# The high and low parts of two FFN weights, made and stored in earlier stages of a two-layer FFN kernel

## The chip, the cores and the metric

The kernel runs on one core of one Trainium2 chip. The metric is the device time of one execution in microseconds (us). The engines of the core are named as in the profile: PE is TensorE (matmuls and transposes), PEld its weight loads, DVE is VectorE, ACT is ScalarE, POOL is GpSimd, and SP is SyncE, which here issues nearly all DMAs, in the order of its own instruction list. Every engine takes its instructions in order: an instruction that waits holds all that stand behind it on its engine.

## The reference

The input is 2 x 1024 rows of 1024 numbers in float32. There are two layers, each followed by a residual addition and a layer norm. The first is a gated FFN in which, of each row's 2752 gate values, the 1376 of least magnitude are set to zero. The second is a gated FFN with weights that are repeated four times and have a small correction of rank 2.

```python
s = silu(x @ w_gate.T)                      # 2048 x 2752
s = s with the I/2 smallest |s| of each row set to 0
x = layernorm(x + (s * (x @ w_up.T)) @ w_down.T)

def lin(x, wq, A, B):                       # w = tile(wq, (1, 4))
    return x @ w.T + (x @ A.T @ B.T) * 0.5
h = silu(lin(x, w1q, a1, b1)) * lin(x, w3q, a3, b3)
x = layernorm(x + lin(h, w2q, a2, b2))
```

## The kernel before

**Tiles and precision.** The 2048 rows are 16 tiles of 128 rows, in four groups of four. A float32 operand is split into a high part (a cast to the rounded type fp32r, on ACT, line 172) and a low part (operand minus high part, on POOL or DVE, line 173), and a product is made of three matmuls: high by high, high by low, low by high. A weight that several groups use is split once; its parts are stored to device memory, and later groups load the two parts instead of the raw weight.

**Stages, in order of time.** `gate_up` makes the gate and up products of all groups. `topk` finds each row's threshold by a search that counts on ACT and DVE; the counting of a group runs beside the matmuls of later work, and that of the last group runs during `down`. `down(g)`, for g from 0 to 3, makes the down product of one group, the residual and the layer norm. It is a loop over six stretches of the 2752 columns (512, 512, 512, 384, 384, 448) and the four tiles of the group, 24 items in all. `ffn(g)` then makes the second layer of one group: f1, eight blocks of 344 hidden columns by four tiles (the four repeated quarters of the weight allow it to work on the rows folded to 256 columns), and f2, the product with w2.

**An item of down.** `item` (the call in `down`) issues the loads of an item, does its preparation two items later and its matmuls three items after that. The loads are m (the gate times up values, line 699), u (the mask of the topk, line 700) and, at the first item of a stretch, the stretch's weight rows (`down_w`): either stored parts (line 673) or a raw row (line 600) that is split. ACT turns u to bf16 (701), POOL multiplies m by it (702), PE transposes m (723), ACT and DVE make the high and low parts mh and ml of the transposed tile (727, 728), and the matmuls run at line 743. DVE adds their sum to acc (746), which frees the PSUM buffer. After a tile's last stretch the layer norm runs on DVE with one instruction on POOL (y, line 577), and the tile goes to device memory (765).

**The critical section.** At the end of a topk DVE reads a flag and may branch to an exact search. Around that branch all engines have a branch of their own, DVE waits there for the work that was issued earlier, DMAs too, and no DMA is issued by SP in the meantime. The last of these sections falls into down(2).

**f1 and its weights.** `f1_prep` gets for each block the parts wh and wl of w1 and w3, 344 KB each, from four buffers of each kind. In group 0, `cached` loads the raw weight to a ring of three buffers (`wr`, which the rows of w_down and w2 use also), splits it, with the low part of w3 on DVE and that of w1 on POOL, and `cache_put` stores both parts; groups 1 to 3 load the parts. The five rows of w2 go the same way in f2. A block's matmuls are lines 959 to 962, its epilogue is silu on ACT (965), the product on DVE (966), the products with a2 (pa, DVE 968) and their sums (ACT 970), and on POOL the sum of the folded quarters (hf, 972). Before a tile's f1 its rows are folded on POOL (905 to 907), and fold and the small tile tl are transposed on PE (927, 929). `ffn_consts` and `f1_first` prepare the first FFN group's constants and tiles during down(3).

**Order.** The Python code gives the order in which instructions are recorded; a scheduler then orders each engine's list by a timeline of its own and the pools' free buffers. `load_behind()` keeps a load behind the last load of down on SP, and `behind()` keeps an instruction behind the last mh and ml on ACT and DVE. Generators such as `topk`, `dots_down` and `ffn_consts` are advanced a step at a time by the items of `down`.

Of the kernel before, what the change touches and what calls it, by code (L numbers as in the profile page):

```python
# [7 lines left out]
F = mybir.dt.float32  # L8
R = mybir.dt.float32r
# [4 lines left out]
ALU = mybir.AluOpType  # L14
# [4 lines left out]
P = 128  # L19
# [5 lines left out]
BW = 344  # L25
NB = NI // BW
# [6 lines left out]
GT = 4  # L33
# [32 lines left out]
class Kern:  # L66
# [7 lines left out]
    def run(self):  # L74
        tc, nc = self.tc, self.nc
        nt = self.nt
        ng = nt // GT
        with ExitStack() as es:
# [51 lines left out]
            self.acc = Ring("acc", [(self.dp2, f"acc{i}", H) for i in range(5)] + [(dp3, f"acc{i}", H) for i in range(5, 8)], F)  # L130
            for r, n in ((self.wh, "wh"), (self.wl, "wl")):
                r.slots += [(self.wp2, n + "x", H), (self.dp2, n + "y", H), (dp3, n + "z", H)]
            list(self.d0)
            for g in range(1, ng - 1):
                list(self.down(g))
            list(self.dg)
            for r in (self.acc, self.wh, self.wl):
                r.drop(dp3)
# [275 lines left out]
    def topk(self, g, nact=3):  # L414
        nc, tk, sm = self.nc, self.tk, self.sm
        V = nc.vector
        tiles = range(g * GT, (g + 1) * GT)
        row = lambda n, dt=F, bufs=2: sm.tile([P, GT], dt, tag="k" + n, bufs=bufs, name=n)
# [4 lines left out]
        b = ku.rearrange("p a n -> p (a n)").bitcast(F)  # L423
        jk = tk.tile([P, NI], U8, tag="jk", name="jk")
        asum, d = row("asum"), row("d")
        lo, hi, cur = pair("lo"), pair("hi"), pair("cur")
# [23 lines left out]
        for p in range(NPASS):  # L450
            for j in range(nact):
# [3 lines left out]
                with self.behind():  # L455
                    t, s = cur[:, 0, j : j + 1], cur[:, 1, j : j + 1]
                    nc.scalar.activation(jk.bitcast(I8), av[j], AF.Sign, bias=t, scale=-1.0, accum_out=s)  # L457
                    if m < GT:
                        t, s = cur[:, 0, m : m + 1], cur[:, 1, m : m + 1]
# [14 lines left out]
            t = nxt[:, 0]  # L474
# [36 lines left out]
                    kv[j], av[j], thr[:, j : j + 1], None, ALU.is_ge, ALU.add, accum_out=cnt[:, j : j + 1]  # L511
                )
        yield
        bad, fl, ft = row("bad"), sm.tile([P, 32], F, tag="kfl", bufs=1, name="fl"), sm.tile([P, 32], F, tag="kft", bufs=1, name="ft")
        V.tensor_scalar(bad, cnt, float(NI - KZ), None, ALU.not_equal)
        V.memset(fl, 0.0)
        V.tensor_reduce(fl[:, 0:1], bad, mybir.AxisListType.X, ALU.max)
# [1 line left out]
        fr, f4 = sm.tile([P, 1], F, tag="kfr", bufs=1, name="fr"), sm.tile([1, 4], F, tag="kf4", bufs=1, name="f4")  # L519
# [85 lines left out]
    def down(self, g, f1=None, early=0):  # L605
        n = 0
        for ib in range(len(DB)):
            if f1 is not None:
                if ib == f1:
                    self.fg = self.f1_first()  # L610
            ws = []
            for t in range(g * GT, (g + 1) * GT):
                st = {"e": n} if n < early else {}
                load = lambda: self.down_load(st, ib, t, n)
                prep = lambda st=st, ib=ib: self.down_prep(st, ib)
                mm = lambda st=st, ib=ib, t=t, ws=ws: self.down_mm(st, ib, t, ws)
                if n < early:
                    load()
                    prep()
                    self.q2.append(mm)  # L620
                    if n == early - 1:
                        yield
                else:
                    self.item(lambda: (load(), self.down_w(g, ib, ws)), prep, mm, 2, 3)
                n += 1
                if g == 0 and n == 12:
                    self.tkg = self.topk(self.nt // GT - 1, 2)
                if (n > 11 or g) and self.tkg and next(self.tkg, 1):
                    self.tkg, self.dg = None, self.dots_down()
                if f1 is not None and n > 4:  # L630
                    next(self.fcg, None)
                    if ib >= f1:
                        next(self.fg, None)
                for _ in range(2 if n % 2 else 1):
                    next(self.dg, None)
        if f1 is not None:
            list(self.fg)
        yield
# [180 lines left out]
    def ffn_consts2(self):  # L819
        nc, fp2, A = self.nc, self.fp2, self.A  # L820
        self.c2 = True
        self.c2h = fp2.tile([P, H], R, name="c2h")
        self.c2l = fp2.tile([P, H], R, name="c2l")
        raw = self.wr.get()
        nc.gpsimd.memset(raw[96:P, :H], 0.0)
        nc.sync.dma_start(raw[0:48, :H], A["w2t"][640:688, :])
        nc.sync.dma_start(raw[48:96, :H], A["w2t"][640:688, :])
        for i in range(2):
            nc.sync.dma_start(raw[96 + 2 * i : 98 + 2 * i, :H], A["b2t"])
        self.split(self.c2h, self.c2l, raw[:, :H])  # L830

    def ffn(self, g):
        tiles = [t for t in range(g * GT, (g + 1) * GT) if t < self.nt]
        for b in range(NB):
            ws = []
            if tiles[-1] + 1 < self.nt:
                if b % 2 == 0:
                    if b:
                        self.f1_tile2(tiles[-1] + b // 2)
                    self.f1_tile(tiles[-1] + 1 + b // 2)  # L840
            for t in tiles:
                self.item(
                    lambda: self.f1_prep(b, ws),
                    lambda: None,
                    lambda st=self.fst[t], b=b, ws=ws: self.f1_mm(st, b, ws),
                    2, 2,
                )
        if tiles[-1] + 1 < self.nt:
            self.f1_tile2(tiles[-1] + GT)
        ws = []  # L850
        for t in tiles:
            self.item(
                lambda: self.f2_w(ws),
                lambda t=t: self.f2_prep(self.fst[t], t),
                lambda st=self.fst[t], t=t, ws=ws: self.f2_mm(st, t, ws),
                2, 1,
            )
# [212 lines left out]
```

## Time and profile before

| what | us |
|---|---|
| three runs | 1931.73, 1930.43, 1925.01 |
| their median | 1930.43 |
| the profiled execution | 1929.24 |
| its span in the trace | 1927.4 |
| TensorE busy in the span | 1885.9 |
| DMA engines, share of the span | 71.9% |

The page cuts the span into 40 equal slices of 48.2 us. Each digit is a share in tenths (9 is 90% or more); the row PEclk is the clock that TensorE was granted.

```profile
PE   9999999999999999999999999999999999998998
DVE  4633555767358474691237996778558757779565
PEclk9999999999999999999999999999999999999999
DMA  7667697676967868667797756877776878485661
GB/s 270 236 248 262 231 328 259 214 274 253 331 227 244 313 243 297 233 221 255 277 345 271 281 188 233 308 254 261 280 240 248 269 285 322 157 317 177 226 199 66
```

By the first and last matmuls of each kind in the trace, gate_up ends at 933 us, down(0) to down(3) run from there to 1471, and the four FFN groups from 1467 to 1919: f1 of group 0 until 1553, its f2 until 1594, f1 of group 1 until 1665, and so on. So a stage is several slices long, and its numbers are read from windows of its own.

### The profile page before, as it was taken

The page shows a single profiled execution, that of the slowest core. Times are in us where ns is not written, and L with a number is a line of the kernel's source. Part 1 is how long each engine was busy: PE and PEld are TensorE (multiplying, and loading weights), DVE is VectorE, ACT ScalarE, POOL GpSimd, SP SyncE. Part 2 cuts the span into 40 slices and gives each one's busy share as a digit, 9 for nine tenths or more (in the row PEclk, how much of TensorE's full clock was granted, in tenths as well). Part 3 has the DMA queues.
Part 4 walks back from the last instruction along what each step waited for, and adds up shares of the span by engine and source line. Part 5 has one row for each costly group of instructions (what it writes and reads, how often), then busy time and mean ns, then how long its engine had stood idle before and what let it go on. Part 6 is the DMA issues. An engine that isn't in the chain of part 4 may idle for free. (4 is left out here: it accounts for less than half of the span.)

```text
span 1927.4 us, 29369 instructions
## 1 busy us (share of the span) xinstructions
PE 1885.9 (98%) x10825; PEld 1755.3 (91%) x10825; DVE 1229.5 (64%) x1831; ACT 905.5 (47%) x1448; POOL 974.0 (51%) x606
## 2 busy tenths in 40 slices
PE   9999999999999999999999999999999999998998
PEld 9999999999999999999887887788877979898896
DVE  4633555767358474691237996778558757779565
ACT  4333478414882258612246532323333746567362
POOL 5665664435445354355555543545655746436062
PEclk9999999999999999999999999999999999999999
DMA  7667697676967868667797756877776878485661
GB/s 270 236 248 262 231 328 259 214 274 253 331 227 244 313 243 297 233 221 255 277 345 271 281 188 233 308 254 261 280 240 248 269 285 322 157 317 177 226 199 66
DMA packets 166205, 488.66 MB, mean 254 GB/s; under 512 B 24772, under 2 KB 45380, under 8 KB 166056
## 3 DMA queue, kind: packets, MB, share of 16 engines
q1 hardware_dynamic: 165848, 486.43, 71.9%
q8 instruction: 85, 1.39, 0.3%
q14 instruction: 64, 0.52, 0.1%
q10 hardware_dynamic: 208, 0.31, 0.0%
HBM read 370.30 MB, written 116.33 MB: 252 GB/s over the span
## 5 line engine op out<-in xcount | busy, mean ns | idle before, releaser
L173 POOL TENSOR_TENSOR wl<-wr,wh 128x1376 fp32r<-128x1376 f32 (+2 forms) x187 | 566.7, 3038 | 430.1 <-ACT wh L172 411.7
L350 PE MATMUL mm<-wh,xh 128*128 128x344 f32 x1928 | 611.1, 322 | 3.5 <-DMA wh<-tw3T1h 3.5
L350 PE MATMUL mm<-wh,xl 128*128 128x344 f32 x1928 | 610.4, 320 | 0.0
L172 ACT CAST wh<-wr 128x1376 fp32r<-128x1376 f32 (+2 forms) x192 | 232.1, 1215 | 300.7 <-PE mm L350 181.7
L350 PEld LDWEIGHTS mm<-wh,xh 128*128 128x128 f32 x1928 | 365.0, 189 | 4.0 <-issue 3.7
L350 PEld LDWEIGHTS mm<-wh,xl 128*128 128x128 f32 x1928 | 364.9, 189 | 0.0
L350 PE MATMUL mm<-wl,xh 128*128 128x344 f32 x1928 | 342.4, 320 | 0.0
L350 PEld LDWEIGHTS mm<-wl,xh 128*128 128x128 f32 x1928 | 310.6, 188 | 0.0
L743 PE MATMUL mm<-wh,mh 128*128 128x512 f32 x680 | 221.1, 404 | 9.1 <-ACT mh L727 3.9
L743 PE MATMUL mm<-wl,mh 128*128 128x512 f32 x680 | 213.9, 395 | 0.9 <-POOL wl L173 0.9
L743 PE MATMUL mm<-wh,ml 128*128 128x512 f32 x648 | 204.4, 396 | 0.0
L702 POOL TENSOR_TENSOR m<-m,ub 128x512 f32<-128x512 f32 (+2 forms) x93 | 111.2, 1196 | 177.9 <-DMA m<-m_d 107.2
L457 ACT ACTIVATE jk<-a,cur 128x2752 int8<-128x2752 f32 x66 | 170.8, 2588 | 41.7 <-DVE cur L487 24.8
L972 POOL TENSOR_TENSOR hf<-hf,gt 128x344 f32<-128x344 f32 x96 | 142.5, 1494 | 73.3 <-DVE gt L966 66.4
L959 PE MATMUL mm<-wh,fh 128*128 128x344 f32 x512 | 166.0, 325 | 7.2 <-DVE gt L966 6.8
L961 PE MATMUL mm<-wh,fl 128*128 128x344 f32 x512 | 164.1, 320 | 0.0
L960 PE MATMUL mm<-wl,fh 128*128 128x344 f32 x512 | 163.9, 320 | 0.0
L746 DVE TENSOR_TENSOR acc<-acc,mm 128x1024 f32<-128x1024 f32 x96 | 116.5, 1215 | 74.3 <-PE mm L743 49.5
L743 PEld LDWEIGHTS mm<-wl,mh 128*128 128x128 f32 x680 | 128.4, 189 | 30.3 <-POOL wl L173 1.7
L743 PEld LDWEIGHTS mm<-wh,mh 128*128 128x128 f32 x680 | 123.5, 189 | 34.5 <-ACT mh L727 5.0
L743 PEld LDWEIGHTS mm<-wh,ml 128*128 128x128 f32 x648 | 121.4, 189 | 26.8
L970 ACT ACTIVATE pa<-pa 128x344 f32<-128x344 f32 x256 | 123.0, 483 | 44.5 <-DVE pa L968 39.0
(191 smaller groups left out, 2735.8 us busy)
## 6 DMA issues: line engine op xcount, KB each, us to landing
wr<-wu SPq DMA_DIRECT2D x64, 688.0 KB
wr<-wg SPq DMA_DIRECT2D x52, 688.0 KB
wr<-wd SPq DMA_DIRECT2D x48, 512.0 KB
s_d<-cc SPq DMA_DIRECT2D x64, 344.0 KB
m_d<-mt SPq DMA_DIRECT2D x64, 344.0 KB
a<-s_d SPq DMA_DIRECT2D x64, 344.0 KB
wl<-wc_w SPq DMA_DIRECT2D x48, 344.0 KB
wh<-wc_w SPq DMA_DIRECT2D x48, 344.0 KB
```

The lines of the kernel that those rows point to most:

```text
L172: self.lasta = self.nc.scalar.copy(hi, raw)
L173: (eng or self.nc.gpsimd).tensor_tensor(lo, raw, hi.bitcast(F), ALU.subtract)
L350: self.nc.tensor.matmul(o, l, r, start=start and n < m and n % (2 * KH) == 0, stop=stop and n >= m and (n - m) % KH == KH - 1)
L457: nc.scalar.activation(jk.bitcast(I8), av[j], AF.Sign, bias=t, scale=-1.0, accum_out=s)
L702: nc.gpsimd.tensor_tensor(m[:, :w], m[:, :w], ub[:, :w], ALU.mult)
L743: nc.tensor.matmul(ps[:, h], a, b[:, h * 512 : (h + 1) * 512], start=i == 0, stop=i == len(ops) - 1)
L746: nc.vector.tensor_tensor(out, out, ps.rearrange("p a b -> p (a b)"), ALU.add)
L959: nc.tensor.matmul(o, fh[:, c, :], wh[:, c, :], start=c == 0, stop=False)
L960: nc.tensor.matmul(o, fh[:, c, :], wl[:, c, :], start=False, stop=False)
L961: nc.tensor.matmul(o, fl[:, c, :], wh[:, c, :], start=False, stop=False)
L970: nc.scalar.activation(pa[:, r], pa[:, r], AF.Copy, scale=0.5, accum_out=part[:, r, b : b + 1])
L972: G.tensor_tensor(hf[:, hs], hf[:, hs], gt, ALU.add)
```

## The change

A generator `ffn_parts` goes over the eight blocks of w1 and w3, sixteen jobs. A job is a load of the raw block to a tile fr, a cast to fh on ACT with the low part on POOL (written over fr), and the two stores; each of the three is a step. The generator is made after down(0) and advanced once by each of the 24 items of down(1) and of down(2), 48 steps. The tiles fr and fh have one buffer each, in a pool that is closed after down(2). The parts then stand in the cache when `f1_prep` asks for them in group 0, so `cached` returns after two loads. A small tile of topk takes another tag (line 514 before).

```diff
--- before.py
+++ after.py
@@ -130,9 +130,14 @@
             self.acc = Ring("acc", [(self.dp2, f"acc{i}", H) for i in range(5)] + [(dp3, f"acc{i}", H) for i in range(5, 8)], F)
             for r, n in ((self.wh, "wh"), (self.wl, "wl")):
                 r.slots += [(self.wp2, n + "x", H), (self.dp2, n + "y", H), (dp3, n + "z", H)]
+            fw_es = ExitStack()
+            self.fwp = fw_es.enter_context(tc.tile_pool(name="fwp", bufs=1, side="right", reuse_waits="tile"))
             list(self.d0)
+            self.fwg = self.ffn_parts()
             for g in range(1, ng - 1):
                 list(self.down(g))
+            list(self.fwg)
+            fw_es.close()
             list(self.dg)
             for r in (self.acc, self.wh, self.wl):
                 r.drop(dp3)
@@ -511,7 +516,7 @@
                     kv[j], av[j], thr[:, j : j + 1], None, ALU.is_ge, ALU.add, accum_out=cnt[:, j : j + 1]
                 )
         yield
-        bad, fl, ft = row("bad"), sm.tile([P, 32], F, tag="kfl", bufs=1, name="fl"), sm.tile([P, 32], F, tag="kft", bufs=1, name="ft")
+        bad, fl, ft = row("bad"), sm.tile([P, 32], F, tag="kfl", bufs=1, name="fl"), sm.tile([P, 32], F, tag="kdf8", bufs=2, name="ft")
         V.tensor_scalar(bad, cnt, float(NI - KZ), None, ALU.not_equal)
         V.memset(fl, 0.0)
         V.tensor_reduce(fl[:, 0:1], bad, mybir.AxisListType.X, ALU.max)
@@ -627,6 +632,8 @@
                     self.tkg = self.topk(self.nt // GT - 1, 2)
                 if (n > 11 or g) and self.tkg and next(self.tkg, 1):
                     self.tkg, self.dg = None, self.dots_down()
+                if 0 < g < self.nt // GT - 1:
+                    next(self.fwg, None)
                 if f1 is not None and n > 4:
                     next(self.fcg, None)
                     if ib >= f1:
@@ -828,6 +835,22 @@
         for i in range(2):
             nc.sync.dma_start(raw[96 + 2 * i : 98 + 2 * i, :H], A["b2t"])
         self.split(self.c2h, self.c2l, raw[:, :H])
+
+    def ffn_parts(self):
+        nc = self.nc
+        job = [(k, b) for b in range(NB) for k in ("w1", "w3")]
+        for k, b in job:
+            raw, hi = (self.fwp.tile([P, 2, BW], dt, tag=t, name=t) for t, dt in (("fr", F), ("fh", R)))
+            with self.load_behind():
+                nc.sync.dma_start(raw, self.A[k][b])
+            yield
+            with self.behind():
+                nc.scalar.copy(hi, raw)
+                nc.gpsimd.tensor_tensor(raw.bitcast(R), raw, hi.bitcast(F), ALU.subtract)
+            yield
+            with self.load_behind():
+                self.cache_put((k, b), hi, raw.bitcast(R))
+            yield
 
     def ffn(self, g):
         tiles = [t for t in range(g * GT, (g + 1) * GT) if t < self.nt]
```

## The prediction

> **What bounds the kernel now.** I read the page first, then the busy time of each engine by stage, then who waited for whom where TensorE has holes. The page:
>
> ```profile
> span 1927.4 us, 29369 instructions
> PE 1885.9 (98%) x10825; PEld 1755.3 (91%) x10825; DVE 1229.5 (64%) x1831; ACT 905.5 (47%) x1448; POOL 974.0 (51%) x606
> ```
>
> TensorE is the bound and the change takes no matmul away. So only its holes (41.5 us of the span), and the half-clock time that follows a hole, can be won or lost. The stage table says where they are; its windows follow the last use of each kind of matmul in the timeline (columns: window, its length, busy us of each engine with its count, granted clock, DMA share, GB/s).
>
> ```profile
> core 0: us, PE busy (x) PEld busy (x) DVE busy (x) ACT busy (x) POOL busy (x), PEclk, DMA share, GB/s
> 1055.00:1190.00 135.00, 135.00 (x638) 110.70 (x637) 126.05 (x179) 58.74 (x80) 60.47 (x49) 1.00 0.67 230
> 1190.00:1322.00 132.00, 127.35 (x584) 103.57 (x583) 100.66 (x144) 39.51 (x61) 64.39 (x46) 0.97 0.79 279
> ...
> 1410.00:1472.00 62.00, 59.10 (x271) 47.62 (x270) 46.24 (x93) 16.44 (x26) 32.94 (x41) 0.97 0.80 263
> 1472.00:1556.00 84.00, 75.38 (x459) 72.40 (x458) 68.45 (x104) 57.84 (x174) 61.53 (x48) 0.98 0.81 279
> 1556.00:1591.00 35.00, 33.96 (x149) 27.14 (x150) 15.54 (x40) 9.70 (x24) 7.18 (x15) 0.95 0.65 254
> 1591.00:1666.00 75.00, 74.30 (x476) 73.69 (x474) 55.29 (x105) 48.23 (x160) 49.31 (x43) 1.00 0.78 279
> ```
>
> Rows one and two are most of down(1) and down(2), where the change puts work; row three is the end of down(3); rows four and five are f1 and f2 of FFN group 0, which makes its own parts; row six is f1 of group 1, which loads them. For each I count idle (length less PE busy) plus clock (length times what is missing from 1.00): down(2) 4.65 + 4.0 = 8.6; end of down(3) 2.9 + 1.9 = 4.8; f1 of group 0 8.6 + 1.7 = 10.3; its f2 1.0 + 1.75 = 2.8; group 1 0.7, and 0.1 in its f2 (32.91 of 33.00), 0.8 in all. The stretch that the change relieves loses 17.9 us, its loaded twin 0.8. What ended the holes, 1410 to 1562 us (total, times, longest):
>
> ```profile
> ACT wh L172 <- DMA wr<-w: 11.7, 3, 5.8
> ...
> PE mm L959 <- DVE gt L966: 3.3, 3, 2.3
> ...
> PE mm L743 <- ACT hh L1006: 3.0, 1, 3.0
> ```
>
> The first is ScalarE held by a raw w1 or w3 that hasn't landed, with mh L727 of down behind it; the next two are VectorE and ScalarE late with group 0's epilogues. Their reason, in f1 of group 0 (two rows) and of group 1 (one row; busy us, mean ns):
>
> ```profile
> L968 DVE TENSOR_TENSOR pa<-gt,ab 128x688 f32<-128x688 f32 x22 | 27.1, 1233 | 0.8
> ...
> L173 DVE TENSOR_TENSOR wl<-wr,wh 128x688 fp32r<-128x688 f32 x6 | 8.6, 1428 | 8.2 <-ACT wh L172 8.2
> ```
> ```profile
> L968 DVE TENSOR_TENSOR pa<-gt,ab 128x688 f32<-128x688 f32 x23 | 21.0, 912 | 0.9
> ```
>
> VectorE does six subtractions of w3 there (8.6 us), waits 8.2 us before them, and its pa L968 is 0.32 us longer each than in group 1: the long ones (2.79 us at 1551.9) lie beside a GpSimd subtraction.
>
> **The change, part by part.** Moved are sixteen jobs: one load of 344 KB on SP, one cast on ScalarE (0.76 us, the 128x688 form of L172), one subtraction (1.67 us on GpSimd; eight were on VectorE, now all are on GpSimd), two stores of 344 KB. Added: 32 loads of parts in group 0, of which the built order puts eight at the start of down(3) and the rest between the f1 blocks, as in groups 1 to 3. The w2 splits and the second constants stay, but the built order moves them to the end of down(3), where w1 and w3 stood.
>
> (a) Mid-f1 waits for gt: 3.3 us. VectorE loses 8.6 us of subtractions, ScalarE 16 x 0.76 = 12.2 us of casts (four before 1455, the others up to f1's end), and GpSimd 13.4 us (eight at 1.67), which shortens pa. I leave 0.3, as group 1 has hardly any: -3.0 (bounds 0 and -3.3).
> (b) Start of f2: the 3.0 us wait for hh, 0.6 for hl after it, and 1.75 of clock, 5.4 together; w2 subtractions stood between the last epilogues on VectorE (at 1546.4 and 1555.9) and go. Group 1 loses 0.8 there: -4.6 (bounds -2 and -5.4).
> (c) Transposes of fold at the start of f1: some 2.4 us idle (waits for fold L907 and tl L918 of 1.9, 0.4 and 0.1) and 1.7 of clock. No w1 or w3 subtraction lies on GpSimd in 1460 to 1483, so their removal doesn't cure this; but the new PE order puts fourteen f1 matmuls (14 x 0.157 = 2.2 us) ahead of two of these transposes. Half: -2.0 (bounds 0 and -4.1).
> (d) End of down(3), 4.8 us. ScalarE no longer waits for raw w1 and w3, but w2's casts (1.05 us each, behind 512 KB loads) stand there now. Half: -2.4 (bounds +4, ScalarE stuck as long again, and -4.8).
> (e) The critical section after the last topk, in down(2), 1180 to 1215 us:
>
> ```profile
> DVE z L579 <- POOL y L577: 6.6, 3, 5.6
> ...
> PE mm L743 <- DVE ve L575: 3.7, 1, 3.7
> ```
>
> SP issued nothing from 1180.7 to 1187.7; m came late (GpSimd waited 13.4 us for four of them), its y stood behind two such m, VectorE waited 5.6 us for y with the acc L746 behind it that frees PSUM, then TensorE stopped. The new order puts y behind one m, which helps; it also puts 344 KB + 512 KB more ahead of the section (2.1 us at the 412 GB/s of the fullest 10 us slice), a cast and a subtraction. I take -1.0 (bounds +6 and -8.6).
> (f) The jobs in down(1) and down(2). GpSimd gets 16 x 1.67 = 26.7 us on its 124.9 of 267, ScalarE 12.2 on 98.3, SP 48 issues at about 0.4 us, the DMA engines 48 x 0.352 MB = 16.9 MB, 41 us at 412 GB/s: the share goes from 0.73 to 0.88. Cover: the transposes run three items (about 5.6 us each) ahead of their matmuls, and TensorE was never idle in 1055 to 1190. Each job adds waits: its stores wait for the cast and the subtraction, and the next load for both stores since there is one buffer; behind them on SP stand m and u of down. The cast waits for its load, behind it mh L727; behind the subtraction stand m L702 and wl. Without the cover a late wl or m stops TensorE at once (0.9 us at 1208). I take +2.5, three such stops (bounds 0 and the slower rival's price).
>
> Sum: -3.0 - 4.6 - 2.0 - 2.4 - 1.0 + 2.5 = -10.5. The profiled execution took 1929.24 us (span 1927.4), so 1918.7, and I say 1919; the median of the runs, 1930.43, lies 1.2 above it, which is inside their spread of 6.7.
>
> A rule that speaks against the change: the Trainium skill, "SBUF — State Buffer", section "SBUF: two separate sides", says that VectorE and GpSimd share one port pair as an exclusive lock, so that a GpSimd instruction blocks a VectorE one with two SBUF inputs for its whole length. The lengthened pa beside GpSimd agrees with it (1233 against 912 ns). In down(1) VectorE is busy 126 of 135 us; if each of the sixteen subtractions blocked it for its 1.67 us and all came through to TensorE, the sum would be +26.7 instead of +2.5, 1943 us. But most of VectorE's instructions there read one operand from PSUM or have one input, so I keep to the rows.
>
> **The rivals.**
> Nearly no gain, 1925: w2 takes w1's place at the transition, so that (c) and (d) give nothing and (e) neither, and (f) costs its 2.5: -3.0 - 4.6 + 2.5 = -5.1, 1924.1. For it: the same ring wr and the same in-order ScalarE. Against: less data in all at the transition.
> More gain, 1909: group 0 becomes like group 1 (17.9 - 0.8 = 17.1) and (f) is hidden, with 3 us out of (e): -20.1. For it: TensorE's faultless 135 us in down(1). Against: (c) has causes of its own.
> Slower, 1942: SP's order. A store that isn't ready holds all loads behind it; the trace has one such hold, in SP's timeline:
>
> ```profile
> 1437.69 0.34 SPq L699 DMA_DIRECT2D m<-m_d  x1
> 1445.20 0.32 SPq L876 DMA_DIRECT2D wc_w<-wh  x1
> ```
>
> For 7.2 us nothing was issued, until the cast of 1444.4. With 32 such stores among m, u and wd in a stage at 0.88 of the DMA engines, a hold longer than the lead of the loads does what (e) did, 8.6 us. Three of them: -13.0 + 25.8 = +12.8. It decides from 22.7 / 8.6 = 2.6 holds. Against it: the lead of three items is about 17 us, more than twice that hold.
> That parts aren't used is excluded by the built order: 48 steps at two times 24 items are the sixteen jobs, and all 32 loads of group 0 are there.
>
> **How the numbers follow.** Forecast 0.38 (own range 1912 to 1920.5), more gain 0.14, nearly no gain 0.28, slower 0.20. A change below 0.5% (9.65 us, so from 1920.8 to 1940.1) can't be told from none by a measurement of this kernel: faster 0.38 + 0.14 = 0.52, same 0.28, slower 0.20. The range goes from 1907, which leaves out the best of the gain (0.06), to 1938, which leaves out most of the slower case (0.14).
>
> **What would show it.** After it: f1 and f2 of group 0 with at most 5 us idle; no wait of TensorE for gt in its middle and pa L968 near 0.9 us (a, b); fold still named at its start (c); ScalarE waiting for wr<-w2t in place of wr<-w (d); VectorE's wait for y below 2 us after the section (e); windows of down(1) and down(2) with at most 8 us idle together and a DMA share near 0.88 (f). The prediction is wrong if TensorE waits in down for m, wl or mh for more than 8 us, or if the transition keeps its 10 us.

## The result: slower, and the profile after

| | median us (lowest to highest) | runs | ratio to before |
|---|---|---|---|
| before | 1931.73 (1925.01 to 1932.83) | 5 | |
| changed | 1945.55 (1943.73 to 1946.78) | 5 | 1.008 [1.0065, 1.0096] |

Forecast was 1919 with a range up to 1938; the changed kernel is 0.8% slower, some 14 us. The profiled execution took 1946.78 us. Its page:

```profile
span 1944.8 us, 29444 instructions
PE 1893.2 (97%) x10825; PEld 1763.2 (91%) x10825; DVE 1219.2 (63%) x1823; ACT 907.7 (47%) x1448; POOL 993.5 (51%) x614
```

TensorE makes the same 10825 matmuls and transposes but is busy 7.3 us longer (some of it at half clock), and its holes grew from 41.5 to 51.6 us. The stage table of the changed kernel (columns as before; the rows follow its own stages: most of down(1), down(2) from the critical section, two halves of down(3), then f1 and f2 of FFN group 0):

```profile
core 0: us, PE busy (x) PEld busy (x) DVE busy (x) ACT busy (x) POOL busy (x), PEclk, DMA share, GB/s
1060.00:1195.00 135.00, 131.34 (x609) 106.63 (x606) 127.05 (x164) 62.05 (x87) 76.78 (x55) 0.99 0.82 280
1195.00:1325.00 130.00, 122.67 (x568) 100.03 (x569) 99.10 (x143) 42.13 (x66) 74.32 (x52) 0.99 0.90 327
1325.00:1410.00 85.00, 80.53 (x359) 64.76 (x358) 48.56 (x85) 24.91 (x36) 37.83 (x32) 0.96 0.83 302
1410.00:1482.00 72.00, 67.41 (x317) 54.99 (x316) 49.37 (x96) 22.44 (x40) 48.13 (x53) 0.98 0.69 228
1482.00:1575.00 93.00, 84.94 (x503) 81.68 (x501) 63.83 (x119) 53.42 (x164) 56.01 (x48) 0.93 0.70 244
1575.00:1609.00 34.00, 33.23 (x153) 26.51 (x153) 17.88 (x48) 9.17 (x24) 5.27 (x15) 1.00 0.43 149
```

Count idle plus clock as the prediction did. Down(1), faultless before, loses 3.7 + 1.35 = 5.0. Down(3), rows three and four, loses 4.5 + 4.6 idle and 3.4 + 1.4 clock = 13.9, where the end of down(3) lost 4.8 before, and the 88 us ahead of it 0.1:

```profile
1322.00:1410.00 88.00, 87.90 (x414) 71.67 (x414) 57.06 (x98) 31.43 (x50) 50.62 (x46) 1.00 0.74 260
```

The start of f2 is cured: row six loses 0.8. But f1 (row five) loses 8.1 + 6.5 = 14.6 by this count, more than the 10.3 of before, though group 0 no longer splits anything there. Who waited for whom, in that order of the stages (total us, times, longest):

```profile
DVE z L584 <- POOL y L582: 3.2, 4, 1.4
...
ACT br L177 <- DMA m<-m_d: 11.1, 1, 11.1
...
POOL fold L928 <- PE tp L950: 9.8, 1, 9.8
...
PE tp L950 <- POOL fold L930: 7.6, 3, 3.5
```

Line one is the y of the critical section, which was 5.6 and is 1.4 at the longest. Line two is new: ScalarE held for 11.1 us by a small constant of the FFN (br) with mh and wh of down behind it. Lines three and four are a loop: GpSimd waits for TensorE's transposes, then TensorE for GpSimd's fold. In TensorE's timeline (start, us, what, idle before):

```profile
1498.74 0.69 PE L950 MATMUL tp<-ident,fold 128*128 128x128 f32 x2 [1.96 <-POOL fold L930]
...
1502.00 0.69 PE L950 MATMUL tp<-ident,fold 128*128 128x128 f32 x2 [2.14 <-POOL fold L930]
...
1506.64 0.69 PE L950 MATMUL tp<-ident,fold 128*128 128x128 f32 x2 [3.53 <-POOL fold L930]
```

Three folds are transposed with no f1 matmul between. Fold has one buffer, so GpSimd can begin the next only after each transpose; in the third round it also waited 2.3 us for the load of the rows (x2a). From the first of these transposes on TensorE is granted half clock for 13.65 us. The count above takes half of that, 6.8 us, but TensorE stood idle for 5.7 us of it, in the last two holes, so the clock itself costs 4.0 and f1 loses some 12 in all.

### The profile page after: what moved, and what is told of

Read it like the earlier page. It is cut to its first block, busy times and chain, and to the rows that moved or that the text cites. A ratio compares the mean times of both kernels' runs of the same rounds, so it can differ in the third digit from the quotient of the medians.

```text
span 1944.8 us, 29444 instructions
## 1 busy us (share of the span) xinstructions
PE 1893.2 (97%) x10825; PEld 1763.2 (91%) x10825; DVE 1219.2 (63%) x1823; ACT 907.7 (47%) x1448; POOL 993.5 (51%) x614
## 5 line engine op out<-in xcount | busy, mean ns | idle before, releaser
L178 POOL TENSOR_TENSOR wl<-wr,wh 128x1376 fp32r<-128x1376 f32 (+1 forms) x179 | 551.4, 3089 | 446.6 <-ACT wh L177 410.4
L177 ACT CAST wh<-wr 128x1376 fp32r<-128x1376 f32 (+1 forms) x176 | 220.2, 1256 | 301.3 <-PE mm L355 181.5
L750 PE MATMUL mm<-wh,mh 128*128 128x512 f32 x680 | 221.8, 405 | 14.6 <-ACT mh L734 7.5
```

What stands on the lines that cost most here:

```text
L177: self.lasta = self.nc.scalar.copy(hi, raw)
L178: (eng or self.nc.gpsimd).tensor_tensor(lo, raw, hi.bitcast(F), ALU.subtract)
L750: nc.tensor.matmul(ps[:, h], a, b[:, h * 512 : (h + 1) * 512], start=i == 0, stop=i == len(ops) - 1)
```

## The experiments

Each kernel was timed beside runs of before on the same chip; ratios are to those, with a 95% interval. For the place of a loss I use one count over all profiles: the time from down's first matmul to its k-th (of 2008), and on to the first matmul of f2 of groups 0 and 1, less the same time of before. One profiled execution each: half-clock stretches (1.7 us) and the critical section (3 us between two kernels of one order) move single values, and in jobs_dma, jobs_cmp and hold_after the profiled execution is the longest of its kernel, 5.1, 4.8 and 5.4 us over the median. In changed, late_loads and hold_after twelve more f1 matmuls (1.9 us) stand ahead of down's last matmul than before, so there the end of down(3) holds a little of f1.

| kernel | ratio [interval] | first stretch of down(1) | end of down(1) | end of down(2) | end of down(3) | f2, group 0 | f2, group 1 |
|---|---|---|---|---|---|---|---|
| changed | 1.0080 [1.0065, 1.0096] | +4.2 | +7.2 | +7.5 | +17.8 | +16.6 | +14.7 |
| jobs_only | 1.0065 [1.0046, 1.0084] | +5.0 | +5.3 | +5.6 | +11.9 | +11.2 | +11.6 |
| jobs_dma | 1.0054 [1.0035, 1.0072] | +4.9 | +6.2 | +6.5 | +14.3 | +13.2 | +12.7 |
| jobs_cmp | 1.0041 [1.0021, 1.0061] | +4.2 | +7.8 | +8.1 | +11.9 | +10.9 | +11.1 |
| tiny_jobs | 1.0015 [1.0001, 1.0029] | -0.1 | -0.2 | +0.1 | +1.7 | +1.7 | +2.4 |
| tag_only | 1.0023 [1.0011, 1.0035] | +1.6 | +4.9 | +5.2 | +5.7 | +5.9 | +5.6 |
| loads_only | 0.9983 [0.9970, 0.9995] | +1.7 | +1.1 | +1.1 | +6.3 | +0.1 | -1.7 |
| late_loads | 1.0053 [1.0036, 1.0070] | +4.8 | +7.9 | +8.2 | +13.0 | +11.6 | +9.7 |
| hold_after | 1.0044 [1.0028, 1.0060] | +6.2 | +8.4 | +8.9 | +21.9 | +13.7 | +11.6 |
| hold_before | 1.0039 [1.0024, 1.0053] | 0.0 | -0.8 | -0.8 | -0.1 | +2.9 | +9.1 |
| pin_tag | 1.0051 [1.0032, 1.0070] | +8.5 | +10.1 | +10.3 | +9.8 | +9.9 | +10.1 |
| pin_jobs | 1.0094 [1.0072, 1.0115] | +8.4 | +5.8 | +7.6 | +15.0 | +13.9 | +13.2 |
| early | 1.0005 [0.9992, 1.0018] | +0.2 | -0.3 | -0.1 | +5.0 | -1.4 | -3.3 |

### Are the jobs free?

**jobs_only**: the changed kernel, its parts stored under other names, so that FFN group 0 splits its own weights as before.

```diff
-                self.cache_put((k, b), hi, raw.bitcast(R))
+                self.cache_put(("spare_" + k, b), hi, raw.bitcast(R))
```

> All sixteen jobs run in down(1) and down(2) as in the changed kernel, but nobody reads their parts: group 0 of the FFN splits its own weights as before. Theory A (the loss has two sources, the jobs' own work in down(1) and down(2), and the earlier part loads at the transition): against before +6 to +8 us, with the holes near 1091 (3.4 us with its clock) and 1195 to 1221 (11 against 8 us) there, and down(3), f1 and f2 as before; ratio 1.003 to 1.004. Rival B (the work in down(1) and down(2) is the whole of it, and shifts what follows): +14 or more, ratio above 1.007. Rival C (the jobs are free, everything is lost at the transition): within 2 us of before.

1943.36 against 1931.17, +12.2 us: the jobs, with the edit of the tag that they carry here, cost nearly the whole of the loss, more than theory A said. By the table half of it falls in down(3), where theory A had nothing. The stage rows for down(1) and down(2):

```profile
1060.00:1195.00 135.00, 131.34 (x614) 106.00 (x613) 131.41 (x170) 63.90 (x87) 74.76 (x57) 1.00 0.82 287
1195.00:1325.00 130.00, 125.70 (x581) 102.19 (x580) 98.79 (x139) 43.48 (x66) 74.48 (x52) 0.99 0.91 327
```

VectorE is busy 131 of 135 us, the DMA engines at 0.91 in down(2). How a job reaches TensorE is seen in GpSimd's timeline after the critical section, where nothing is ahead:

```profile
1213.16 1.18 POOL L709 TENSOR_TENSOR m<-m,ub 128x512 f32<-128x512 f32 x1 [4.11 <-DMA m<-m_d]
1214.29 1.68 POOL L849 TENSOR_TENSOR fr<-fr,fh 128x688 fp32r<-128x688 f32 x1
1215.92 2.35 POOL L178 TENSOR_TENSOR wl<-wr,wh 128x1024 fp32r<-128x1024 f32 x1
```

m is 4.1 us late, the job's subtraction (line two) stands between it and wl, and TensorE waits 2.3 us for that wl at 1218.3.

**tiny_jobs**: the same with 8 of 344 columns. **jobs_dma**: the bytes without the compute. **jobs_cmp**: the compute without the bytes (tiles made once and cleared).

```diff
  tiny_jobs
-            raw, hi = (self.fwp.tile([P, 2, BW], dt, tag=t, name=t) ...
+            raw, hi = (self.fwp.tile([P, 2, 8], dt, tag=t, name=t) ...
-                nc.sync.dma_start(raw, self.A[k][b])
+                nc.sync.dma_start(raw, self.A[k][b][:, :, :8])
  jobs_dma
-                nc.scalar.copy(hi, raw)
+                nc.scalar.copy(hi[:, :, :8], raw[:, :, :8])
...
-                self.cache_put(("spare_" + k, b), hi, raw.bitcast(R))
+                self.cache_put(("spare_" + k, b), raw, raw)
  jobs_cmp
-                nc.sync.dma_start(raw, self.A[k][b])
+                nc.sync.dma_start(raw[:, :, :8], self.A[k][b][:, :, :8])
...
-                self.cache_put(("spare_" + k, b), hi, raw.bitcast(R))
+                self.cache_put(("spare_" + k, b), hi[:, :, :8], raw.bitcast(R)[:, :, :8])
```

> The same 48 steps with 8 columns in place of 344: the same instructions on SP, ScalarE and GpSimd in nearly the same places, TensorE's order that of before but for eight places, and almost no bytes and no work. Nobody reads the parts. If the jobs cost by their bytes and busy time: within 2 us of before. If they cost by their waits and their places in the queues (a store that holds SP until its subtraction is done): as much as jobs_only, +6 or more.

> As jobs_only, but the cast and the subtraction of a job take 8 columns of 344, and both stores carry the raw tile (nobody reads them, the result doesn't change): all the bytes, no compute. Theory D (the 16.9 MB in a stage that is already at 0.66 to 0.77 of the DMA engines make m, u and the wd rows late): at least 8 of the 12.5 us of jobs_only, ratio 1.004 or more, with POOL and ScalarE waiting for m, u and wr. Theory C (the subtractions of 1.67 us on GpSimd and the casts on ScalarE, which stand between m, wl and mh): within 4 us of before, as tiny_jobs (1.0015).

> As jobs_only, but loads and stores carry 8 columns of 344, and cast and subtraction work on a full tile that stays in SBUF: all the compute, nearly no bytes. Theory C: at least 8 of the 12.5 us of jobs_only, ratio 1.004 or more, TensorE waiting for wl of GpSimd. Theory D: within 4 us of before, as tiny_jobs (1.0015).

1.0015, 1.0054, 1.0041. All three carry the edit of the tag, which alone costs 1.0023 (below), so the 32 extra instructions and 48 issues with their waits cost nothing that shows. The program with the bytes is some 0.0031 to 0.0039 (6 to 7.5 us) over the controls tag_only and tiny_jobs, that with the compute 0.0018 to 0.0026 (3.5 to 5 us); the intervals of jobs_cmp and of the controls overlap, so the second is not clear of the noise. Neither theory alone holds. Beside the stops of the critical section, which tiny_jobs and before have too, jobs_dma adds stops of TensorE for ml and ub (2.5 and 1.2 us) and jobs_cmp for m and ml (2.3 and 1.4): I read them as the lead of the transposes running out, with bytes alone or compute alone.

**pin_tag, pin_jobs**: the built order of the changed kernel lets three ml pass, then puts two acc in a row on VectorE, where before the two alternate but for two early pairs of ml. To part order from work, TensorE's transposes and matmuls and VectorE's ml and acc keep the recorded order in down(1) and down(2), once without jobs (on tag_only) and once with (on jobs_only).

```diff
+    def pinned(self, last):
+        return self.tc.issue_after(last.ins) if self.pin and last is not None else ExitStack()
...
+        with self.pinned(self.pe):
             for c in range(nf):
-                nc.tensor.transpose(...)
+                self.pe = nc.tensor.transpose(...)
```

> The control for pin_jobs: tag_only with the order of TensorE's transposes and matmuls and of VectorE's ml and acc fixed in down(1) and down(2) to the order in which they are recorded (transposes, matmuls, transposes, matmuls). No jobs. Expected within 5 us of tag_only on either side; what counts is the difference to pin_jobs.

> jobs_only with the same fixed order as pin_tag. In jobs_only, jobs_dma and jobs_cmp the scheduler, which counts the jobs in, lets ml and acc run in other orders in the first stretch of down(1) and at the end of down(1) (three ml ahead, then two acc in a row) than in before, and there the stops are. If the new order costs and not the work: pin_jobs within 4 us of pin_tag. If the jobs' bytes and busy time cost in any order: 7 to 12 us over pin_tag, as jobs_only over tiny_jobs (9.7).

1940.91 (1.0051 [1.0032, 1.0070]) and 1949.42 (1.0094 [1.0072, 1.0115]): 8.5 us apart, as jobs_only lies 0.0042 (8.1 us) over tag_only. With the order of down(1) and down(2) fixed the jobs cost the same by the medians, so a new order there isn't what costs. Two of pin_jobs' six runs are at 1943 and four at 1949 to 1950, and the profiled one is of the two, so where these 6 us lie isn't seen.

Order in down(3) is a rival that stays open, and there most of the price falls. At the end of down(2) jobs_only is 0.4 us behind tag_only, at the end of down(3) 6.2; pin_jobs goes from 2.7 ahead of pin_tag to 5.2 behind. Yet in jobs_only the jobs' last store is issued at 1334, ahead of down(3)'s first matmul at 1347. Holes of down(3), with the clock's share of the busy time, come to 4.7 us before, 4.5 in tag_only, 5.7 in tiny_jobs, 3.7 in pin_tag and 7.8 in jobs_cmp, in all of which TensorE has the same order there; they come to 11.2 in jobs_only, 11.9 in jobs_dma and 11.9 in pin_jobs, where the scheduler put its transposes and matmuls in another. TensorE's waits from 1325 to 1478, in jobs_only (two lines) and in tag_only:

```profile
PE tp L950 <- POOL fold L930: 3.5, 2, 2.5
PE tp L730 <- DVE fl L956: 2.4, 1, 2.4
...
PE tp L927 <- POOL fold L907: 1.7, 3, 0.8
...
PE tp L723 <- DVE fl L933: 1.0, 1, 1.0
```

No run holds the order of down(3) fixed, so whether the bytes cost by themselves or through that order isn't shown.

### The transition to the FFN

**loads_only**: the kernel before, without jobs; all w1 and w3 tiles are loaded from stored parts of the same size (those of w_down, so the output isn't the reference's).

```diff
+        if key[0] in ("w1", "w3"):
+            for w, d in zip((wh, wl), self.wd_d[0]):
+                nc.sync.dma_start(w.bitcast(F), d[:, : 2 * BW].rearrange("p (a b) -> p a b", a=2))
+            return
```

> No jobs at all: from group 0 on, the w1 and w3 tiles are two loads of stored parts of the same bytes (other data, rows of w_down's parts, in all groups and blocks, so the output isn't the reference's). Theory A: the FFN gains what the changed kernel's group 0 gained and loses at the transition (end of down(3) about 12 us of holes with clock against 5, fold and transposes at the start of f1 about 14 against 5), so -5 to +4 us against before. Rival (the losses at the transition are an echo of the jobs): down(3) and the start of f1 no worse than before and the whole 10 us of the mid-f1 and f2 holes gone, so -8 to -12 us, ratio 0.994 to 0.996.

1927.63 against 1931.17, -3.5 us. This is what the change brings in this order when the parts cost nothing: the FFN gains 8.0 us (+6.3 to -1.7 in the table), and down(3) gives back 5.2.

**late_loads**: the changed kernel with its part loads behind the last load of down.

```diff
         if key in self.cache:
-            for w, d in zip((wh, wl), self.cache[key]):
-                nc.sync.dma_start(w.bitcast(F), d)
+            with self.load_behind():
+                for w, d in zip((wh, wl), self.cache[key]):
+                    nc.sync.dma_start(w.bitcast(F), d)
```

> The changed kernel, but every load of a w1 or w3 part stands behind the last load of down on SP, as the raw loads of the jobs do. If the part loads that were put ahead at the start of down(3) are what made ScalarE wait 11.1 us for the small constants' load (br) with mh and wh behind it: down(3) back to some 5 us of holes with clock, and 5 to 7 us less than the changed kernel (ratio to before about 1.004 to 1.005). If the constants are late for another reason: within 2 us of the changed kernel, ratio 1.007 to 1.009.

1942.07, which is 3.5 us under the changed kernel by the medians and 0.0027 (5 us) by the ratios, whose intervals just overlap. Its rows of down(3) are clearer:

```profile
1325.00:1410.00 85.00, 82.60 (x386) 66.78 (x385) 61.93 (x104) 28.95 (x44) 47.66 (x40) 1.00 0.80 286
1410.00:1478.00 68.00, 62.98 (x297) 50.82 (x296) 41.04 (x77) 18.89 (x32) 41.20 (x46) 1.00 0.82 285
```

7.4 us of holes and full clock, against 13.9. ScalarE's longest wait for br fell from 11.1 to 5.8 us, and the changed kernel's stops of 4.2 and 3.2 us at 1400 and 1441 are gone:

```profile
PE mm L750 <- ACT mh L734: 4.6, 3, 3.2
PE mm L750 <- ACT wh L177: 4.2, 1, 4.2
```

The changed kernel issues eight parts (2.8 MB) between 1346 and 1372, 110 us ahead of f1; here they go out between 1454 and 1459, 20 us ahead, and nothing waits for them. That down(3) loses 6.5 us less with the parts behind is shown, in one profile; TensorE's order there changes with the edit too, and that the constants queued behind the early parts on the DMA engines is my reading of the order in time. Of the 10.3 us that the changed kernel falls back in down(3) by the table, late_loads keeps 4.8, and jobs_only, which loads no parts at all, has 6.3.

**hold_after, hold_before**: the transposes of the next group's rows may not pass the f1 matmul recorded before them. The built order had all four of them (tiles 4 to 7, first used in group 1) at the start of f1 of group 0 or just before, in before as in the changed kernel; with this edit they stand after one, three, five and seven of its eight blocks, and nothing of down moves.

```diff
-        for c in range(2):
-            nc.tensor.transpose(tp[:, c, :], f[:, c * P : (c + 1) * P], self.ident)
+        with self.tc.issue_after(self.lastf.ins) if t >= GT else ExitStack():
+            for c in range(2):
+                nc.tensor.transpose(tp[:, c, :], f[:, c * P : (c + 1) * P], self.ident)
...
```

> The changed kernel with the same edit. In the changed kernel three of these transposes stand back to back at 1498 to 1507, 7.6 us of holes and 13.6 us at half clock (6.8 us lost). If my reading is right that they are needless there: 10 to 14 us less than the changed kernel, which is 1931 to 1936 us, within 0.3% of before. If TensorE would have to wait there for something else (part loads, epilogues of f1): less than 4 us gained, ratio to before above 1.005.

> The kernel before, with one edit: the transposes of the rows of the next group (fold and tl of tiles 4 to 7 and so on) may not be moved ahead of the f1 matmul that was recorded last before them. In before four such groups of transposes stand at the start of f1 of group 0 in TensorE's list, 80 us before they are needed, each waiting for a fold of GpSimd. If they are what costs the 4.1 us of step (c): 3 to 5 us less than before, ratio 0.9975 to 0.9985, no wait for fold between 1475 and 1490. If something else stands ready to take their place (the first matmuls have to wait for the epilogues of down's last tiles anyway): within 1.5 us of before.

The changed kernel gains 7 us (1938.22, 1.0044 against 1.0080), less than the 10 to 14 expected, but in line with the finer count: f1 now loses 4.2 + 1.7 = 5.9 in place of some 12.

```profile
1485.00:1572.00 87.00, 82.83 (x505) 80.64 (x504) 62.71 (x120) 53.43 (x164) 53.81 (x48) 0.98 0.77 264
```

The kernel before loses 7 us by the same edit (1936.54, 1.0039 [1.0024, 1.0053]). TensorE's waits in its group 0:

```profile
PE mm L960 <- DVE hf L967: 4.5, 3, 2.5
PE tp L1005 <- DVE fl L934: 2.9, 1, 2.9
PE mm L743 <- ACT hh L1007: 2.0, 1, 2.0
```

Where VectorE still splits w3 there, TensorE is only sent sooner into waits for VectorE, at the end for the next group's fl too. That is 2.9 of the 9.1 us that the profile is behind at f2 of group 1; the rest comes after the start of f2 of group 0, with waits for hl (1.4 us) and, ahead of group 1's matmuls, for VectorE's sum x (2.6). The same transposes fill time in the one kernel and hold TensorE up in the other.

### The edit that issues nothing

**tag_only**: the kernel before with the changed tag of one tile of 128 bytes. Every engine's instructions and order are those of before. **pad_up**: its own tag, 128 bytes wider.

```diff
  tag_only
-sm.tile([P, 32], F, tag="kft", bufs=1, name="ft")
+sm.tile([P, 32], F, tag="kdf8", bufs=2, name="ft")
  pad_up
-sm.tile([P, 32], F, tag="kft", bufs=1, name="ft")
+sm.tile([P, 64], F, tag="kft", bufs=1, name="ft")[:, :32]
```

> The kernel before with nothing but the changed kernel's edit of the small tile's tag: the same instructions in the same order on every engine, but 128 bytes a partition less in the pool of small tiles, so that wh and wl of gate_up lie 128 bytes lower. In the profiles so far gate_up's matmuls follow one another by 157.5 ns in the three programs without this edit and by 158.05 ns in the eleven with it, before any job runs. If the edit is the cause: 158.0 ns here, gate_up 3 us later (5784 x 0.55 ns), ratio 1.001 to 1.002. If something else of the changed programs is: 157.5 ns and within 1 us of before.

> The kernel before with the small tile's tag kept and made 128 bytes wider instead of given up: the same instructions in the same order, wh and wl of gate_up 128 bytes higher than in before, where tag_only has them 128 bytes lower. If it is the place of the tiles in SBUF that sets the pace of gate_up's matmuls, another pace than 157.5 ns is likely; if places 256 bytes apart are alike, the pace of tag_only, 158.0 ns, and a ratio of 1.001 to 1.003. If it is the shared tag itself (a wait for a buffer) and not the place: 157.5 ns and within 1 us of before.

tag_only is 1934.04 against 1929.59, ratio 1.0023. The same 700 us of gate_up in before, tag_only and pad_up:

```profile
100.00:800.00 700.00, 700.00 (x4447) 700.00 (x4446) 399.70 (x531) 371.94 (x318) 352.84 (x107) 1.00 0.75 264
```
```profile
100.00:800.00 700.00, 700.00 (x4430) 700.00 (x4430) 393.63 (x528) 370.47 (x317) 352.05 (x107) 1.00 0.75 263
```
```profile
100.00:800.00 700.00, 700.00 (x4431) 700.00 (x4430) 398.36 (x526) 370.71 (x318) 352.44 (x107) 1.00 0.75 263
```

TensorE is busy throughout at full clock, but makes 17 matmuls fewer. Start to start they take 157.49 ns in before and 158.04 in the other two, over 5784 matmuls 3.2 us. The first buffer of wh in gate_up begins at byte 37088 of a partition in before, at 36960 in tag_only and 37216 in pad_up. So it is the place, not the shared tag; the changed kernel has 36960 and 158.04 ns too. Pad_up's time, 1.0010 [0.9999, 1.0020], is below the 1.0017 that the pace alone would give; its critical section ran shorter.

### A version that beats both

**early**: the jobs in gate_up of groups 1 to 3, where TensorE waits but once (3.5 us near 880), as 32 half jobs. **early_late**, **early_hold**, **early_hold_late** add the edits above.

```diff
             if g and (u, w, k) == TKAT:
                 self.tkg = self.topk(g - 1)
+            if g:
+                next(self.fwg, None)
...
-                if 0 < g < self.nt // GT - 1:
-                    next(self.fwg, None)
```

> The jobs moved out of down into gate_up of groups 1 to 3 (32 half jobs of 128x344, one of its 96 steps with each of gate_up's steps), where TensorE is busy 600 of 600 us between 100 and 700, GpSimd half idle and the DMA engines at 0.73; FFN group 0 loads the parts as in the changed kernel. If the 12.5 us of jobs_only are the price of their place beside the topk and the critical section of down(1) and down(2): what is left is loads_only, 1 to 6 us less than before, ratio 0.997 to 0.9995, with down(1) and down(2) within 2 us of before. If the jobs cost that much wherever they stand: above 1.003.

> As early, and the part loads of w1 and w3 behind the last load of down, as in late_loads. Late_loads was 3.5 us under the changed kernel; if that gain stands by itself: 3 to 4 us under early. But in its order three transposes of the next group stand back to back at the start of f1, as in the changed kernel, so rather within 2 us of early: what down(3) wins, f1 gives back.

> As early, and the transposes of the next group kept behind the f1 matmul recorded before them, as in hold_before and hold_after. In the changed kernel, where VectorE and GpSimd have no splits left in f1, this took the chain away and gained 7 us; here two of four stand at the start, with 4.5 us of holes and 1.7 of clock. If VectorE is free enough: 3 to 6 us under early, ratio 0.994 to 0.997. If VectorE's late epilogues take their place, as in hold_before: within 2 us of early.

> As early, with both edits. If both gains stand, the best of the four: 8 to 12 us under before, ratio 0.9935 to 0.996. If down(3) is slow for its order of ScalarE's and GpSimd's work and not for the early loads: as early_hold.

1.0005 [0.9992, 1.0018], 1.0030 [1.0016, 1.0044], 0.9989 [0.9975, 1.0003] and 0.9989 [0.9979, 1.0000]. Early's down(1) and down(2):

```profile
1060.00:1195.00 135.00, 135.00 (x637) 110.55 (x636) 124.08 (x174) 57.72 (x80) 59.26 (x48) 1.00 0.67 229
1195.00:1325.00 130.00, 125.82 (x578) 102.11 (x577) 102.54 (x146) 39.49 (x61) 64.80 (x45) 0.97 0.79 278
```

They are those of before again. Early_late has the three transposes in a row, 9.0 us of holes for fold: f1 loses there more than the late loads win in down(3), as was half expected. With both edits the gain is smaller than hoped.

**early_hold_kft, early_hold_late_kft**: the same with the tile's own tag, as before had it; order unchanged.

> As early_hold (jobs in gate_up, transposes of the next group held back), with the small tile's own tag given back as in before; every engine's order is that of early_hold. If the tag and the 128 bytes cost 3 us in gate_up: 157.5 ns between matmuls, 3 us under early_hold, ratio to before 0.9965 to 0.998, faster than both kernels. If not: as early_hold, 0.9975 to 1.0003.

> As early_hold_late (jobs in gate_up, transposes of the next group held back, part loads behind down's last load) with the small tile's own tag. If the 3 us of gate_up's pace are won here: 0.9965 to 0.998, faster than both kernels. If, as in early_hold_kft, a faster gate_up runs into waits for its own loads (tw and x parts, beside the jobs' bytes) and gives it back: 0.9985 to 1.0.

157.5 ns again in both. The first is 0.9991 [0.9979, 1.0003]: at the quicker pace TensorE ran into waits in gate_up in its profile (1.9 us for VectorE at 478, 0.9 for a load at 657), about what the pace gains; the other, with the same pace, has neither. The second is 1925.69 against 1931.37, 0.9983 [0.9971, 0.9995]: faster than both kernels, by a sixth of a per cent. Its f1 and f2 of group 0:

```profile
1462.00:1554.00 92.00, 86.06 (x505) 83.66 (x504) 63.37 (x119) 53.58 (x164) 54.06 (x48) 0.94 0.69 236
1554.00:1588.00 34.00, 33.55 (x154) 26.61 (x154) 18.07 (x48) 9.13 (x23) 6.47 (x15) 1.00 0.45 147
```

f1 still loses 11.5 us, to waits for VectorE's hf (5.9 us) and their clock.

## Why the prediction was wrong, step by step

A word on the count first: it takes a hole that lies in half-clock time twice. In down(2) before that is little (holes 4.65 us and 2.9 of clock while busy, 7.6 in place of 8.6, part of it the rounded clock); in f1 of the changed kernel it is 2.9 us.

**(a) Mid-f1 waits for gt, -3.0: right.** None is left in group 0, and pa of gt fell as far as named (1233 ns before); the eight pa of hf rose from 1099 to 1336 ns:

```profile
L991 DVE TENSOR_TENSOR pa<-gt,ab 128x688 f32<-128x688 f32 x23 | 20.3, 883 | 0.8
```

**(b) Start of f2, -4.6: right.** One wait for hh of 0.76 us is left.

**(c) Transposes of fold, -2.0 with bounds 0 and -4.1: wrong in sign.** The step took the fourteen f1 matmuls that moved ahead of two transposes for a help. They pushed these against the third, so that three rounds through the one fold buffer stood in a row: 7.6 us of holes and 4.0 of clock, 11.6 against some 4, so 7.5 more where the step had 2.0 less. The step never asked which rows were being transposed. They belong to the next group, and holding them back gained 7 us (hold_after).

**(d) End of down(3), -2.4 with bounds +4 and -4.8: wrong.** It lost 9 us more. The step looked for what would stand in w1's place on ScalarE and passed over what it had itself noted two paragraphs earlier, that eight of the 32 part loads stand at the start of down(3). Putting them behind down's loads cut down(3)'s loss from 13.9 to 7.4 (late_loads). Part of the loss comes without any part load (jobs_only, 6.3 us), and for that the step has no term.

**(e) Critical section, -1.0: the argument on y was right, the gain did not come.** VectorE's wait for y fell as foreseen. But TensorE now stopped twice for others:

```profile
DVE acc L753 <- DVEq L532: 5.9, 1, 5.9
...
PE tp L730 <- DVE mv L578: 4.7, 1, 4.7
...
PE mm L750 <- POOL wl L178: 2.4, 1, 2.4
```

VectorE stood 5.9 us in the section itself, until 1202.35; its ml behind that ended at 1205.5 and TensorE's transposes, whose wait the profile puts down to mv, began at 1205.6. Row two of the stage table loses 7.3 + 1.3 = 8.6, as much as was there before. One late thing was removed from a section where several are late.

**(f) The jobs, +2.5: mis-sized.** Over tag_only the jobs cost 0.0042 of the time, 8.1 us, three times the estimate; the DMA share came out near what was worked out (0.82 and 0.90 in the two stages, against 0.88 for both). "The transposes run three items ahead" held for TensorE before, in a down(1) without jobs; with them the profile is 4 us behind at the end of the first stretch. And the cost was sought only where the jobs stand, as stops for one late wl or m. But bytes alone cost some three quarters of it, compute alone some two fifths (not clear of the noise), and in the profiles most of the price falls in down(3), behind the jobs. How it comes about there, by the bytes or by the scheduler's other order, stays open.

**A term that was missing.** The edit of the small tile's tag was described and given no price. It is worth 3.2 us by the matmuls' pace, and 4.4 us by the times of tag_only.

**The rivals.** "Slower, 1942" came near in size by another mechanism. SP's holds did not happen: between 1060 and 1330 the longest time in which SP issued nothing is 4.7 us in the changed kernel and 6.1 before (in the critical section 6.3 and 7.0), no store of a job held it for longer than some 4, and tiny_jobs, with the same 32 stores waiting for their casts and subtractions, costs nothing over tag_only. The rule of the Trainium skill ("SBUF — State Buffer", section "SBUF: two separate sides"), by which the sum came to 1943, is near in size too; but as a price for this case it isn't borne out, since the program with all sixteen subtractions and their casts (jobs_cmp) is 3.5 to 5 us over the controls, not 26.7. What it says of pa beside GpSimd fits: 1233 ns with the subtractions there, 883 without.

Together: 4.4 (tag) + 8.1 (jobs) - 3.5 (loads_only, the true size of the benefit, in place of -13.0) + some 5 that the transition costs more than in loads_only. That last part is only the remainder to the measured 14; of the two causes I name for it, the early part loads and the chain, each gained when taken away (3.5 to 5 and 7 us), and the two aren't independent: the FFN's gain would be larger without the chain (10.3 us from the end of down(3) to group 1 in hold_after, 3.1 in the changed kernel).

## What to carry to other kernels

Before pricing a move, price its best case: take the work away altogether and see what comes back. Here it was 3.5 us, so a placement that costs 8 can't pay; placed in a stage where TensorE was busy throughout for 700 us, the same work came out even (early). Look for the price behind the moved work too: a scheduler that counts it in may order the next stage otherwise, and half of what jobs_only lost fell there. Loads that an early result makes possible may be issued early: say behind which load they belong. And an instruction of a later stage that an in-order engine is handed early is free only as long as its input is ready.

## What the runs showed of the hardware

The pace of a faultless stream of matmuls depends on where its tiles lie. With the weight tiles wr, wh and wl 128 bytes lower or higher and the parts of x where they were, 128x344 matmuls of gate_up follow each other by 158.04 instead of 157.49 ns (0.35%), at a granted clock of 1.00, in every one of the programs with either shift (fifteen were profiled) and in none of the five without. The matmuls of f1, whose tiles lie elsewhere, kept 157.2 ns. Which operand it is was not tried. The Trainium skill ("SBUF — State Buffer", section "Operand start alignment") asks only that an operand start at a multiple of its element size and says that its runs timed nothing; all three places satisfy that. The rule is about what is legal, and the difference here is one of speed.
